# Two sparse graph layers on one core: units interleaved by an order that a list of operations makes, over both layers

## The chip, the cores and the metric

The kernel runs on one core of one Trainium2 chip. The metric is the device time of one execution in microseconds, the median of several runs. The profile is one execution on the same kind of chip.

## The reference

There are 2708 nodes with 128 features and a 0/1 adjacency matrix. Its entry (i, j) is drawn with a probability that falls as 1/sqrt((1+i)(1+j)), so the first rows and columns hold most of some 11000 edges. The matrix is dense in memory, 29 MB of float32.

```python
# layer 0: attention over the edges, 4 heads of 32
q, k, v = x @ Wq + bq, x @ Wk + bk, x @ Wv + bv          # by heads
alpha = softmax over the edges of a row of (q . k) / sqrt(32)   # 0 where a row has no edge
out = alpha @ v                                           # by heads, laid out (c, h)
x_r = x @ Ws + bs
beta = sigmoid(concat(out, x_r, out - x_r) @ Wb)
x = layernorm(x + beta * x_r + (1 - beta) * out)
# layer 1: messages over the edges
s, d = x @ msg_w[:, :128].T, x @ msg_w[:, 128:].T
aggregated[i] = sum over edges (i, j) of gelu(s[i] + d[j] + msg_b) * adj[i, j]
h = gelu(concat(x, aggregated) @ upd_w.T + upd_b) + x
x = layernorm(x + layernorm(h) * ln_w + ln_b)
```

## The kernel before

The kernel has a sparse path, `sparse_layers`, and a dense path that runs only if a flag says that some list was too short (more edges in a row or segment than there are slots). The sparse path finds the edges of the adjacency matrix and works edge by edge.

Rows are taken in 22 blocks of R = 126. `plan` cuts the columns of a block into segments in which a row is expected to have few edges, and makes units: block 0 gives three units (a part of the columns each), every other block one, 24 in all. A unit has a number of slots per row (64 in block 0, then 24 or 16) and a number of chunks of 128 edges, 110 in all.

- Start: x is loaded (on the ACT queue), transposed into `xT` by blocks, and multiplied by `wtab`. The result is the table `kv_t` in DRAM, one row of 264 numbers per node: key, and for each head 32 values, a one (for the sum of the weights) and the value's share in the gate.
- `load(b)`: the block's 126 rows of the adjacency matrix come into one of three buffers `abuf` on the SP queue. The buffer's two last partitions hold the column numbers in two parts.
- `keys(b)`: ACT reads the whole buffer as 16-bit numbers to add them up (L654, for the flag). PE multiplies it by `lkey` in pieces of 512 columns (L663), so that each entry is the column number plus 2^20 where there is an edge. The DVE takes the eight largest of each segment (`max`, L667).
- `place(u)`: the candidates of a row are cleaned and sorted by rounds of `max` and `match_replace` (L690, L692). A product with `before` (L696) gives the number of edges in the rows above, so each row owns an interval of edge positions. Two DVE passes (L707, L708) write a 0/1 matrix `t32` whose column e is one where the row owns edge e; ACT casts it to bf16 into `T16` (L710) for later. A product with it (L714) brings each edge its row's query, slots and first position; the DVE picks the slot (L717 to L724) and the index `idx` is there. POOL gathers the rows of `kv_t`, one gather for 128 edges (L728). PE transposes the bf16 matrix (L738), and ACT copies it twice (L741, L742), as `s32` and into `S`.
- `attend(b)`: product of query and key on the DVE (L753), sum by head (L754), exp on ACT (L757), weighted values on the DVE (L759), and a product with `s32` adds them up by row (L765).
- `finish(gi)`: for a group of up to three blocks, division by the sums, gate, residual and layernorm, with a reciprocal square root by shifts and three Newton steps on the DVE (L846 to L852). Then transposes (L816), a product with two weights (L823), a copy to `dv` (L826) that is stored to the table `d_t` in DRAM on the SP queue (L828), and `sv` (L827).
- `message(b)`, layer 1: POOL gathers rows of `d_t` (L906). ACT casts `T16` and `S` back to f32 (L911, L913). A product brings each edge its row's `sv` (L916), the DVE adds (L919), ACT does the gelu (L920), and a product with `s32` adds up by row (L922).
- `update(b, at)`: for each block on its own, two products (L952, L953), gelu, two layernorms with the same Newton steps for one column each (L932 to L939, normalised on the DVE, L947), and a store (L963).

The calls stand in a loop over the blocks (`keys(b)`, then `attend(b - 1)`), then a loop of `update(b, message(b))`. The framework decides the order of the instructions on each engine from that program; each engine then runs its own list in order and waits on semaphores. POOL's queue holds the gathers, SP's the adjacency blocks and the stores of `d_t` and the output, ACT's the stores of `kv_t`.

Of the kernel before, what the change touches and what calls it, by code (L numbers as in the profile page):

```python
# [9 lines left out]
F32 = mybir.dt.float32  # L10
# [5 lines left out]
P = 128  # L16
BANK = 512
# [393 lines left out]

# [6 lines left out]
HV = 34  # L418
RSQRT = float(0x5F3759DF)


def plan(N):

    w = [(1.0 + i) ** -0.5 for i in range(N)]
    total = sum(w)
    units = []
    for b in range(-(-N // R)):
        lam = 4.0 * w[b * R] * N / total  # L430
        edges = 4.0 * N / total * sum(w[b * R : (b + 1) * R])
        n = 3 if b == 0 else 1
        most = min(0.26, 1.4 / lam)
        segments, at, acc = [], 0, 0.0
        for j in range(N):
            acc += w[j] / total
            edge = (j + 1) % KT == 0 or j + 1 == N
            if edge or (acc >= 0.97 * most and j + 1 - at >= CAP and KT - (j + 1) % KT >= CAP and N - j > 64):
                segments.append((at, j + 1, acc))
                at, acc = j + 1, 0.0  # L440
        group, weight = [], 0.0
        for i, (s0, s1, share) in enumerate(segments):
            group.append((s0, s1))
            weight += share
            if i + 1 == len(segments) or (weight >= 0.97 / n and len(units) < n - 1 and b == 0):
                lu, eu = lam * weight, edges * weight
                slots = -(-int(lu + 4.2 * math.sqrt(lu) + 2.5) // 8) * 8
                chunks = int(math.ceil((eu + 3.5 * math.sqrt(eu)) / P))
                units.append((b, group, slots, chunks))
                group, weight = [], 0.0  # L450
    return units
# [3 lines left out]
def sparse_layers(ctx, tc, flag, x, adj, wq, bq, wk, bk, wv, bv, ws, bs, wb, msg_w, msg_b, upd_w,  # L455
                  upd_b, ln_w, ln_b, out):

    nc = tc.nc
    N, D = x.shape
    C = D // HEADS
    NB = (N + R - 1) // R
    scale = 1.0 / math.sqrt(C)
    rows_of = [min(R, N - b * R) for b in range(NB)]
    full = N // R
    units = plan(N)  # L480
    NU = len(units)
    NCH = sum(u[3] for u in units)
    chunk0 = [sum(u[3] for u in units[:i]) for i in range(NU)]
    most_chunks = max(u[3] for u in units)
    most_slots = max(u[2] for u in units)
    TW = D + HEADS * HV
    U16, U32, I32 = mybir.dt.uint16, mybir.dt.uint32, mybir.dt.int32

    def bcast(v, n):
        return v.rearrange("(o d) -> o d", o=1).to_broadcast([P, n])  # L490

    const = ctx.enter_context(tc.tile_pool(name="fconst", bufs=1))
    dram = ctx.enter_context(tc.tile_pool(name="fdram", bufs=1, space=bass.MemoryType.DRAM))
# [3 lines left out]
    xs = const.tile([P, NB, D], F32, name="xs")  # L497
    nc.scalar.dma_start(xs[:R, :full, :], x[: full * R, :].rearrange("(t p) d -> p t d", p=R))
    nc.scalar.dma_start(xs[: N - full * R, full, :], x[full * R :, :])
    wkv = const.tile([P, 2, D], F32, name="wkv")  # L500
    wqs = const.tile([P, 2 * D + 1], F32, name="wqs")
    bkv = const.tile([P, 2, D], F32, name="bkv")
    bqs = const.tile([P, 2 * D + 1], F32, name="bqs")
    nc.scalar.dma_start(wkv[:, 0, :], wk)
    nc.scalar.dma_start(wkv[:, 1, :], wv)
    nc.gpsimd.dma_start(bkv[:, 0, :], bcast(bk, D))
    nc.gpsimd.dma_start(bkv[:, 1, :], bcast(bv, D))
    wb3 = const.tile([P, 3, D], F32, name="wb3")
    nc.gpsimd.dma_start(wb3.rearrange("p a d -> p (a d)"), bcast(wb.rearrange("k o -> (k o)"), 3 * D))
    nc.scalar.dma_start(wqs[:, :D], wq)  # L510
    nc.scalar.dma_start(wqs[:, D : 2 * D], ws)
    nc.gpsimd.dma_start(bqs[:, :D], bcast(bq, D))
    nc.gpsimd.dma_start(bqs[:, D : 2 * D], bcast(bs, D))

    ident = const.tile([P, P], F32, name="fident")
    make_identity(nc, ident)
    ident16 = const.tile([P, P], BF16, name="ident16")
    nc.vector.tensor_copy(ident16, ident)

    lkey = const.tile([P, P], BF16, name="lkey")  # L520
    nc.vector.tensor_scalar(lkey, ident, BIG, None, op0=ALU.mult)

    NADJ = 3
    abuf = [const.tile([P, N], F32, name=f"abuf{i}") for i in range(NADJ)]
    pidx = const.tile([P, 1], F32, name="pidx")
    iota = const.tile([P, most_chunks * P], F32, name="iota")
    dcol = const.tile([P, most_chunks], F32, name="dcol")
    before = const.tile([P, P], BF16, name="before")
    with tc.tile_pool(name="ftmp", bufs=1) as tmp:
        cnum = tmp.tile([1, 2, N], F32, name="cnum")  # L530
        cint = tmp.tile([1, N], I32, name="cint")
        nc.gpsimd.iota(cint, [[1, N]], base=1, channel_multiplier=0)
        nc.vector.tensor_copy(cnum[:, 0, :], cint)
        nc.vector.tensor_single_scalar(cint, cint, 63, op=ALU.bitwise_and)
        nc.vector.tensor_copy(cnum[:, 1, :], cint)
        nc.vector.tensor_sub(cnum[:, 0, :], cnum[:, 0, :], cnum[:, 1, :])
        ones_row = tmp.tile([1, P], BF16, name="ones_row")
        nc.vector.memset(ones_row, 1.0)

        nc.sync.dma_start(lkey[R : R + 1, :], ones_row)  # L540
        nc.sync.dma_start(lkey[R + 1 : R + 2, :], ones_row)
        for a in abuf:
            nc.sync.dma_start(a[R : R + 1, :], cnum[:, 0, :])
            nc.sync.dma_start(a[R + 1 : R + 2, :], cnum[:, 1, :])
        ii = tmp.tile([P, most_chunks * P], I32, name="ii")
        nc.gpsimd.iota(ii, [[1, most_chunks * P]], base=0, channel_multiplier=0)
        nc.vector.tensor_copy(iota, ii)
        di = tmp.tile([P, most_chunks], I32, name="di")
        nc.gpsimd.iota(di, [[P, most_chunks]], base=0, channel_multiplier=1)
        nc.vector.tensor_copy(dcol, di)  # L550
        nc.vector.tensor_copy(pidx, dcol[:, 0:1])

        nc.vector.tensor_scalar(before, iota[:, :P], pidx, None, op0=ALU.is_gt)

    def load(b):
        rows = rows_of[b]
        nc.sync.dma_start(abuf[b % NADJ][:rows], adj[b * R : b * R + rows, :])

    for b in range(NADJ - 1):
        load(b)  # L560

    w_l1 = const.tile([P, 4, D], F32, name="fw_l1")
    nc.gpsimd.dma_start(w_l1[:, 0:2, :], msg_w.rearrange("o (h k) -> o h k", h=2))
    nc.gpsimd.dma_start(w_l1[:, 2:4, :], upd_w.rearrange("o (h k) -> o h k", h=2))
    vecs = const.tile([P, 4, D], F32, name="vecs")
    for i, v in enumerate((msg_b, upd_b, ln_w, ln_b)):
        nc.gpsimd.dma_start(vecs[:, i, :], bcast(v, D))


    xT = const.tile([P, N], F32, name="fxT")  # L570
    bits = const.tile([P, NB], F32, name="bits")
    count = const.tile([P, NU], F32, name="count")
    ends = const.tile([P, NU], F32, name="ends")
    caps = const.tile([P, 2, NU], F32, name="caps")
    for t in (bits, count, ends):
        nc.vector.memset(t, 0.0)
    for u in range(NU):
        nc.vector.memset(caps[:, 0, u : u + 1], float(units[u][2]))
        nc.vector.memset(caps[:, 1, u : u + 1], float(units[u][3] * P))
    idx = const.tile([P, NCH], U32, name="idx")  # L580
    score = const.tile([P, NCH, HEADS], F32, name="score")
    T16 = const.tile([P, NCH * P], BF16, name="T16")
    S = const.tile([P, NCH, R], BF16, name="S")
    sv = const.tile([P, NB, D], F32, name="sv")
    wT = const.tile([P, 4, D], F32, name="fwT")

    wtab = const.tile([P, TW], F32, name="wtab")
    btab = const.tile([P, TW], F32, name="btab")  # L590
    wg = const.tile([P, 2, D], F32, name="wg")
    nc.vector.tensor_add(wg[:, 0, :], wb3[:, 0, :], wb3[:, 2, :])
    nc.vector.tensor_sub(wg[:, 1, :], wb3[:, 1, :], wb3[:, 2, :])
    wA = wg[:, 0, :].rearrange("p (c h) -> p h c", h=HEADS)
    with tc.tile_pool(name="ftmp2", bufs=2) as tmp:
        for src, dst, one in ((wkv, wtab, 0.0), (bkv, btab, 1.0)):
            nc.vector.tensor_copy(dst[:, :D], src[:, 0, :])
            v = src[:, 1, :].rearrange("p (h c) -> p h c", h=HEADS)
            t = dst[:, D:].rearrange("p (h c) -> p h c", c=HV)
            nc.vector.tensor_copy(t[:, :, :C], v)  # L600
            nc.vector.memset(t[:, :, C : C + 1], one)
            pr = tmp.tile([P, HEADS, C], F32, name="pr")
# [407 lines left out]
```

## Time and profile before

| what | value |
|---|---|
| time, median of 3 runs | 802.68 us (801.0 to 806.31) |
| span of the profiled execution, first to last instruction | 778.9 us |
| that execution's own time | the page gives the span alone |
| from the start to the first gather of layer 0 | 88.2 us |
| from there to the first gather of layer 1 | 460.4 us |
| from there to the end | 230.3 us |
| mean granted TensorE clock | 0.616 |

The span runs from the first to the last instruction on the core; the time holds the launch too. Busy time of an engine is the time in which at least one of its instructions ran. "PEld" is the loading of weights into TensorE, which overlaps the products. The granted clock is the share of full speed that TensorE was given. In the list of waits, "POOL g L728 <- DVE rq L690: 99.4, 2, 74.0" reads: the instruction of line 728 on POOL, which writes g, waited 99.4 us in all, 2 times, at the longest 74.0, for the instruction of line 690 on the DVE.

### The profile page before, as it was taken

How to read it: one execution, taken by the hardware profiler on the slowest of the kernel's cores; microseconds unless marked ns; L12 is line 12 of the kernel's file. 1: busy time of each engine (PE TensorE's matmuls, PEld its weight loads, DVE VectorE, ACT ScalarE, POOL GpSimd, SP SyncE). 2: the span in 40 equal slices, each digit the busy share in tenths (PEclk: the TensorE clock that was granted, in tenths of full speed). 3: DMA queues.
4: the chain of work that ended last, by engine and by line, in shares of the span. 5: the costliest groups of instructions: out<-in, count | busy, mean ns of one | idle time of the engine just before them, and what ended most of it. 6: DMA issues, size and time to landing. Idle time of an engine off the chain costs nothing. (4 is left out here: it accounts for less than half of the span.)

```text
span 778.9 us, 6687 instructions
## 1 busy us (share of the span) xinstructions
PE 375.0 (48%) x1416; PEld 266.9 (34%) x1416; DVE 458.3 (59%) x2345; ACT 259.0 (33%) x479; POOL 220.3 (28%) x240
## 2 busy tenths in 40 slices
PE   0367467454546444454454254443456665543310
PEld 0233356233434232233232132332456654433210
DVE  1596787665656555665665545647114543667895
ACT  0293534344424523524523241122243433211000
POOL 5000234332052032032022013030677777340000
PEclk9975556565555565555555556555586776755555
DMA  8346112453143243234234102020122223111000
GB/s 237 112 146 202 54 49 64 137 165 107 29 139 112 75 125 99 77 94 135 78 93 126 34 17 56 11 49 19 42 55 50 61 56 59 34 37 23 14 15 12
DMA packets 24700, 60.29 MB, mean 77 GB/s; under 512 B 5050, under 2 KB 16396, under 8 KB 21940
## 3 DMA queue, kind: packets, MB, share of 16 engines
q0 software_dynamic: 9216, 23.08, 12.9%
q1 hardware_dynamic: 9128, 32.18, 12.9%
q10 hardware_dynamic: 6304, 4.51, 2.0%
q14 instruction: 39, 0.32, 0.1%
q8 instruction: 13, 0.21, 0.1%
HBM read 54.04 MB, written 5.63 MB: 77 GB/s over the span
## 5 line engine op out<-in xcount | busy, mean ns | idle before, releaser
L728 POOL DMA_INDIRECT g<-kv_t,idx x110 | 106.2, 966 | 405.4 <-DVE rq L690 99.4
L906 POOL DMA_INDIRECT gd<-d_t,idx x110 | 103.9, 944 | 80.2 <-issue 31.6
L654 ACT ACTIVATE junk<-abuf 126x5416 uint8<-126x5416 uint16 (+1 forms) x22 | 103.7, 4713 | 51.6 <-DMA abuf<-in_adj_dram 32.0
L663 PE MATMUL pk<-abuf,lkey 128*128 128x512 bf16 x132 | 64.1, 516 | 64.2 <-DVE cand L667 54.3
L765 PE MATMUL pr<-val,s 128*126 128x136 f32 (+1 forms) x220 | 59.7, 436 | 69.0 <-DVE val L759 51.2
L667 DVE MAX8 cand<-pk 128x8 f32<-128x512 f32 (+23 forms) x223 | 87.8, 429 | 0.1
L714 PE MATMUL pq<-rq,t 126*128 126x145 f32 (+3 forms) x220 | 67.8, 467 | 35.1 <-DVE t L708 27.7
L765 PEld LDWEIGHTS pr<-val,s 128*126 128x126 f32 (+1 forms) x220 | 49.6, 309 | 98.8 <-DVE val L759 82.3
L753 DVE TENSOR_TENSOR qe<-qe,g 128x384 f32<-128x384 f32 (+2 forms) x48 | 22.0, 462 | 85.5 <-DMA g<-kv_t,idx 85.4
L919 DVE TENSOR_TENSOR gd<-gd,pz 128x512 f32<-128x512 f32 (+3 forms) x34 | 19.9, 585 | 88.5 <-DMA gd<-d_t,idx 82.6
L916 PE MATMUL pz<-sv,t32b 126*128 126x128 f32 (+1 forms) x220 | 48.4, 375 | 46.9 <-DVE gd L919 30.9
L714 PEld LDWEIGHTS pq<-rq,t 126*128 126x128 f32 (+1 forms) x220 | 53.5, 311 | 45.8 <-DVE t L708 22.3
L916 PEld LDWEIGHTS pz<-sv,t32b 126*128 126x128 f32 (+1 forms) x220 | 41.4, 273 | 53.1 <-DVE gd L919 27.1
L922 PE MATMUL pa<-s32b,gd 128*128 128x126 f32 (+1 forms) x220 | 45.0, 367 | 12.2 <-ACT gd L920 9.7
L922 PEld LDWEIGHTS pa<-s32b,gd 128*128 128x128 f32 x220 | 40.4, 273 | 15.2 <-ACT gd L920 11.8
L663 PEld LDWEIGHTS <-lkey 128*128 128x128 bf16 x132 | 15.3, 122 | 82.9 <-issue 57.4
L920 ACT ACTIVATE gd<-gd 128x512 f32<-128x512 f32 (+3 forms) x34 | 18.6, 548 | 68.8 <-DVE gd L919 65.1
L757 ACT ACTIVATE e<-score 128x12 f32<-128x12 f32 (+2 forms) x48 | 10.0, 220 | 93.5 <-DVE score L754 65.6
L827 DVE TENSOR_TENSOR sv<-pm,vecs 126x128 f32<-126x128 f32 (+1 forms) x22 | 6.4, 291 | 45.5 <-ACT dv L826 45.5
L952 PE MATMUL pn<-fwT,fxT 128*126 128x128 f32 (+1 forms) x44 | 14.6, 436 | 38.1 <-DVE h L955 31.6
L823 PE MATMUL pm<-fwT,fxT 128*126 128x256 f32 (+1 forms) x44 | 23.0, 682 | 20.7 <-ACT fxT L819 20.7
L710 ACT CAST T<-t 126x384 bf16<-126x384 f32 (+3 forms) x48 | 20.0, 437 | 36.2 <-DVE t L708 35.8
(162 smaller groups left out, 756.2 us busy)
## 6 DMA issues: line engine op xcount, KB each, us to landing
abuf<-in_adj_dram SPq DMA_DIRECT2D x21, 1332.8 KB
kv_t<-kv ACTq DMA_DIRECT2D x21, 129.9 KB
g<-kv_t,idx POOLq DMA_INDIRECT x110, 3.0
gd<-d_t,idx POOLq DMA_INDIRECT x110, 2.6
xs<-in_x_dram ACTq DMA_DIRECT2D x1, 1323.0 KB
d_t<-dv SPq DMA_DIRECT2D x21, 63.0 KB
out_dram<-h SPq DMA_DIRECT2D x21, 63.0 KB
abuf<-in_adj_dram SPq DMA_DIRECT2D x1, 655.8 KB
```

The costliest lines, as they stand in the source:

```text
L654: nc.scalar.activation(junk[:rows], a.bitcast(U16)[:rows], AF.Copy, accum_out=bits[:rows, b : b + 1])
L663: nc.tensor.matmul(p[:, :n], lkey, low[:, 2 * c0 + 1 : 2 * (c0 + n) : 2], start=True, stop=True)
L667: nc.vector.max(cand[u][:, i * CAP : (i + 1) * CAP], p[:, s0 - c0 : s1 - c0])
L710: nc.scalar.copy(T16[:rows, (ch + c0) * P : (ch + c0 + m) * P], t32[:rows, : m * P])
L714: nc.tensor.matmul(pq[:, (c - c0) * W : (c - c0 + 1) * W], t32[:rows, (c - c0) * P : (c - c0 + 1) * P], rq[:rows, :W], start=True, stop=True)
L728: nc.gpsimd.indirect_dma_start(out=g[:, c, :], out_offset=None, in_=kv_t[:, :], in_offset=bass.IndirectOffsetOnAxis(ap=idx[:, ch + c0 + c ...
L753: nc.vector.tensor_tensor(qe[:, :m, :], qe[:, :m, :], g[:, :m, :D], ALU.mult)
L765: nc.tensor.matmul(pr[:rows], s32[:, c, :rows], val[:, c, :], start=ch + c == parts[0][0], stop=ch + c == last)
L823: nc.tensor.matmul(pt[:r, : 2 * D], xT[:, b * R : b * R + r], wT[:, 0:2, :].rearrange("p a d -> p (a d)"), start=True, stop=True)
L906: nc.gpsimd.indirect_dma_start(out=g[:, c, :], out_offset=None, in_=d_t[:, :], in_offset=bass.IndirectOffsetOnAxis(ap=idx[:, ch + c : ch + ...
L916: nc.tensor.matmul(pz[:, c * D : (c + 1) * D], t32[:rows, c * P : (c + 1) * P], sv[:rows, b, :], start=True, stop=True)
L922: nc.tensor.matmul(pa[:, :rows], g[:, c, :], s32[:, c, :rows], start=ch + c == mine[0][0], stop=ch + c == last)
```

## The change

`plan` and `sparse_layers` are written anew; the dense path and the switch stay.

- Order. Every operation is first put on a list by `add(engine, ns, function, r=..., w=...)`, with an estimated duration and the names that it reads and writes. `Order.emit` then walks through time: on each engine it takes, of the operations that can start soonest (within 30 ns), the one with the longest chain of estimated work behind it, with 100 ns for each step from one engine to another, and calls the functions in order of the planned starts. The framework keeps that order (`manual_schedule`). The list covers both layers, with fixed buffers and the eight PSUM banks by name; one of them, "MI", is lent to one short step after another.
- Sign steps. Instead of a 0/1 matrix by two DVE passes, `E` is Sign(position + 1/2 - first position of the row), one ACT activation per unit, in f32, with -1 left of the row's first edge and +1 right of it. Everything that is spread over edges by a product with `E` is first turned into differences of neighbouring rows: the slots by a product with `dif`, the queries by `dx` (differences of `xT`'s columns) and half weights, with the bias from a bf16 product of three parts. The row matrix `S32` comes from a product of `E` with `difs` and stays in f32 for both layers; `E` is made again in layer 1. The bf16 copies `T16` and `S`, their transposes and casts are gone.
- Virtual rows. Block 0 has 109 rows. Its 15 heaviest are split by columns into 8 virtual rows each, the next 31 into 4, the next 63 into 2: three units of up to 126 virtual rows, with 32, 24 and 24 slots, and 22 segments in place of 73. The split is a sum of T products over columns t, t + T, ... with shifted copies of `lkey`.
- Groups. Chunks (109) are worked on four at a time across units in `spread`, `attend` and `message`; the selection takes up to 9 chunks at once. Blocks are finished and updated in 9 groups. The table of layer 0 has 260 columns, stored by 7 DMAs; `d_t` and the output are stored by 9 DMAs each. x is loaded first on the SP queue.
- Smaller. In layer 0 the reciprocal square root is exp(-ln/2) on ACT with one Newton step; normalising is done on ACT; the sum of gate and residual and the differences of the new `xT` are done on POOL; in layer 1 the products with `sv`'s weights are made by unit in `skip`.

The core of the diff:

```diff
+HEAVY = ((0, 15, 8), (15, 46, 4), (46, 109, 2))
...
+class Order:
+    HAND = 100.0
...
+                t, p = min(((t, p) for t, p in seen if t <= soon + 30.0), key=lambda s: (-s[1].height, s[1].i))
...
+        for p in sorted(ops, key=lambda p: (p.start, p.i)):
+            p.fn()
...
-                nc.vector.tensor_scalar(after[:rows, : m * P], here, rq[:rows, D + K : D + K + 1], None, op0=ALU.is_ge)
-                nc.vector.scalar_tensor_tensor(t32[:rows, : m * P], here, ends[:rows, u : u + 1],
-                                               after[:rows, : m * P], op0=ALU.is_lt, op1=ALU.mult)
-                nc.scalar.copy(T16[:rows, (ch + c0) * P : (ch + c0 + m) * P], t32[:rows, : m * P])
...
-                    nc.tensor.transpose(pt[:, c * P : c * P + rows], T16[:rows, o : o + P], ident16[:rows, :rows])
...
+        def stepsign(u):
...
+                add("ACT", ac(m * P), lambda c=c, s=s, m=m: A.activation(
+                    E[:, s : s + m, :].rearrange("p c e -> p (c e)"), half[:, c * P : (c + m) * P], AF.Sign,
+                    bias=dsl[:, u.i, 0:1]), r=["half", ("dsl", u.i)], w=[("E", (s + k) % RING) for k in range(m)])
...
+            add("PE", 300, lambda: T_.matmul(mi.ap[:, 2 : 2 + K], dif, rs[:, :K], start=True, stop=True),
+                r=["dif", "dif_", rk], w=[mi])
+            add("ACT", ac(K), lambda: A.copy(dsl[:, i, : K + 2], mi.ap[:, : K + 2]), r=[mi, "dsl"], w=[("dsl", i)])
+            stepsign(u)
...
+                    add("PE", pe(K + 1) + 100, lambda u=u, o=o, c=c: T_.matmul(
+                        view[:, o, :], E[:, (u.c0 + c) % RING, :], dsl[:, u.i, 1 : K + 2], start=True, stop=True),
...
+        def spread(q):
...
+                add("PE", pe(128), lambda j=j, u=u: T_.matmul(
+                    bank[kq][:, j * D : (j + 1) * D], E[:, (c0 + j) % RING, :], dq[u.i % NQ], start=True, stop=True),
...
+                add("PE", pe(R), lambda j=j, sel=sel: T_.matmul(
+                    bank["SS"][:, j * R : (j + 1) * R], E[:, (c0 + j) % RING, :], sel, start=True, stop=True),
...
+            add("ACT", ac(m * R), lambda: A.copy(S32[:, c0 * R : (c0 + m) * R], bank["SS"][:, : m * R]),
...
+            add("POOL", po(n * 128), lambda: G.tensor_tensor(gx[:r, :n, :], gx[:r, :n, :], xs[:r, b0 : b0 + n, :], ALU.add),
...
-        for b in range(NB):
-            if b + NADJ - 1 < NB:
-                load(b + NADJ - 1)
-            keys(b)
-            if b:
-                attend(b - 1)
-        attend(NB - 1)
...
+        for j, bt in enumerate(batches):
+            for u in bt:
...
+                scan(u)
+                place(u)
+            select(j)
+            upto = bt[-1].c0 + bt[-1].nch
+            while 4 * done_q + 4 <= upto or (upto == NCH and 4 * done_q < NCH):
+                spread(done_q)
+                attend(done_q)
+                done_q += 1
...
-    for b in range(NB):
-        update(b, message(b))
...
+        for q in range(-(-NCH // 4)):
+            message(q)
...
+        add.emit({"MI": [bank["MI"]]})
```

## The prediction

> **What bounds the kernel now.** I read the page's head first, then the busy time by stage, then the waits, then single stretches of the timeline. No engine is full:
>
> ```profile
> span 778.9 us, 6687 instructions
> PE 375.0 (48%) x1416; PEld 266.9 (34%) x1416; DVE 458.3 (59%) x2345; ACT 259.0 (33%) x479; POOL 220.3 (28%) x240
> ```
>
> Busy time is the union. The durations of the 2345 DVE instructions add up to 600.3 us, so each overlaps its neighbour by 142.0 / 2345 = 0.061 us; below I take that off every DVE instruction that I count. The median of the runs is 802.68 us, 23.8 us above this execution's span; the page gives no other time for that execution, so I sum against the span and add 23.8.
>
> I cut the span at the first gather of layer 0 (88.2 us) and of layer 1 (548.6 us):
>
> ```profile
> 0.00:88.20 88.20, 39.61 (x109) 21.31 (x109) 49.03 (x258) 36.39 (x30) 10.25 (x20) 0.81 0.52 156
> 88.20:548.60 460.40, 229.73 (x796) 153.24 (x797) 280.10 (x1262) 167.37 (x333) 106.26 (x111) 0.57 0.28 82
> 548.60:778.90 230.30, 105.64 (x514) 92.40 (x513) 129.16 (x826) 55.28 (x119) 103.83 (x110) 0.63 0.18 38
> ```
>
> Columns: window, its length, busy PE, PEld, DVE, ACT, POOL, granted clock, DMA share, GB/s. In layer 0 the DVE is busy 280.1 / 460.4 = 61% and nothing else is busier. The waits say why:
>
> ```profile
> POOL g L728 <- DVE rq L690: 99.4, 2, 74.0
> DVE qe L753 <- DMA g<-kv_t,idx: 85.4, 33, 7.4
> DVE gd L919 <- DMA gd<-d_t,idx: 82.6, 28, 9.1
> DVE sv L827 <- ACT dv L826: 45.5, 22, 14.2
> DVE kk L717 <- PE pq L714: 24.4, 30, 2.7
> ```
>
> The gathers wait for the DVE, which makes the indices, and the DVE waits for the gathers: 85 us in layer 0, although POOL has work for only 106 of 460 us. It is a matter of order. The order is better where many units are at hand, in the densest 60 us of layer 0, with the DVE at 48.75 / 60 = 81%:
>
> ```profile
> 80.00:100.00 20.00, 9.29 (x33) 6.81 (x31) 16.89 (x85) 9.59 (x22) 5.76 (x6) 0.50 0.17 45
> 100.00:120.00 20.00, 13.96 (x53) 11.81 (x54) 16.54 (x78) 7.34 (x28) 7.60 (x8) 0.62 0.23 54
> 120.00:140.00 20.00, 13.35 (x59) 10.30 (x60) 15.32 (x67) 8.28 (x26) 11.87 (x13) 0.73 0.33 81
> ```
>
> Layer 1 has two parts: gathers one after another (a start every 1.25 us, first two lines below), then a tail of updates on the DVE alone:
>
> ```profile
> 571.04 0.94 POOL L906 DMA_INDIRECT gd<-d_t,idx  x1 [0.30 <-issue]
> 572.29 0.94 POOL L906 DMA_INDIRECT gd<-d_t,idx  x1 [0.30 <-issue]
> ...
> 573.24 1.16 PE L916 MATMUL pz<-sv,t32b 126*128 126x128 f32 x8 [2.33 <-DVE gd L919]
> ...
> 636.26 1.91 PE L922 MATMUL pa<-s32b,gd 128*128 128x126 f32 x8
> ...
> 688.27 0.79 PE L952 MATMUL pn<-fwT,fxT 128*126 128x128 f32 x2 [2.31 <-DVE h L955]
> ```
>
> ```profile
> 680.00:778.90 98.90, 28.05 (x106) 22.51 (x104) 75.52 (x531) 8.63 (x23) 11.33 (x12) 0.52 0.09 20
> ```
>
> An f32 product leaves two PE records, so the PE lines price one: 1.16 / 4 = 0.29 us in a row at clock 1.00, 1.91 / 4 = 0.48 at 0.50, 0.79 alone.
>
> **The change: the start.** Before, 88.2 us pass until the first gather: x is queued on ACT while SP has adjacency blocks in flight (its first transpose starts at 23.9), and the 22 rows of the key/value table wait for buffers and for the keys' 73 narrow maxima of block 0. After, x goes first on SP, the adjacency blocks wait for small row transfers, the table rows have room of their own, and its 22 stores on the ACT queue become 7. The DVE has 90 instructions ahead of and including the first index, 32.1 us by the rows (22 table additions at 0.425 are 9.4 of it; a 1x2708 cast of 1.55 becomes 4x677), less 90 x 0.061: 27 us. PE has beside it 22 transposes (5.1 us by L632), 22 table products (20.4 by L641) and the first scans: 32 us. PE cannot begin before x is there. x is 1.39 MB; the first 20 us of before moved 238 GB/s, so 6 us and about 4 until transposed. So the first index is at 10 + 32 + 3 (select) = 45, the first gather at 47. Bounds: 38 (DVE and PE overlap wholly) to 60 (table rows wait as before).
>
> **Layer 0.** Removed: the two interval passes per group of chunks (L707, L708, 17 and 24 us), the cast to T16 (20), the bf16 transposes (L738, 110 products) and their two copies (20 each). Added: one Sign activation per unit for E. No row is a Sign; as an ACT pass of 128x512 it costs 0.61 to 0.63 (L911, L920), so 109 chunks of 128 columns are some 17 us per layer; the ends are 10 and 25. The slots, the queries and the selection then go through difference matrices, which costs PE: 109 products for S, 24 + 24 for slots and queries. The scan is unchanged in width: three virtual units of 2708 columns on PE in place of one, 174 maxima in place of 223, but mostly of the same long segments, so 88 us on the DVE again. Groups of four chunks make 28 rounds of products, scores and values (3 x 0.69 us) in place of 48 smaller ones.
> DVE from the first index to the last val: 652 instructions, 233 us of durations (scan 88, placing 32, selection 20, attention 57, block ends 28, the rest setup), less 40: 193 us, where before has 280.
> PE: 572 f32 products, where before has 286. 439 are 126 to 136 wide, at 0.29 to 0.48: 127 to 211 us. 133 have 16 to 33 columns; no row is so narrow, so half of those prices to all of the upper one: 19 to 64, I take 32 at the half clock. Scans, 127 pieces of 512 columns at 0.28 to 0.53 (L663: 1.06 for two at half clock): 36 to 67. 94 small bf16 products at 0.15 to 0.2: 14 to 19. Sum 196 us at the full clock, 329 at half.
> ACT: 22 reads of the adjacency at 4.9 (L654) are 108, plus Sign 17, copies of S 17 and smaller things: 172. Here is the new wait: the copy of a unit's slots, its Sign and the exp stand in ACT's queue with these reads, and one behind a read holds the PSUM bank MI and PE's next products up to 4.9 us. Uncovered that is 22 x 4.9 = 108 us; other units' maxima and products cover it, as ACT's and DVE's work on other units covers most of the 65.6 us that exp (L757) waits now. POOL: 109 gathers x 1.25 = 136, plus 18 additions and differences that were DVE work. No row is such an addition; between 0.28 (the 128x128 select of the identity) and 1.08 us (the 128x1152 iota, L546) each: 5 to 19, I take 14.
> So the four engines need 193, 196 to 329, 172 and 150 us, and PE's clock decides. Now the clock:
>
> ```profile
> 584.00:588.00 4.00, 2.59 (x12) 0.50 0.33 55
> 588.00:592.00 4.00, 4.00 (x21) 0.50 0.21 52
> 592.00:596.00 4.00, 3.03 (x21) 0.85 0.25 46
> ```
>
> Four full microseconds of PE and the clock rises. With twice the products PE is full more often. I put two thirds of the work at the full clock: about 240 us, and 265 for the stretch (PE 91%, DVE 73%, between its 61% and 81%). Ends: 193 / 0.81 = 238, and PE at half clock, 329 / 0.93 = 354. In the new order of the DVE's instructions 10 to 50 us of its own work lie between an index and the first use of its gather, more than the waits of 7.4 at most, so the 85 us go to nearly nothing; the 45 us for dv go because nobody on the DVE waits for that copy any more.
> The Trainium skill ("TensorE: Matmul & The Clock Gate", section on the HAM clock gate) has a half clock until a window of about 3.4 us is busy, and again after an idle one. The three rows agree. By that rule alone a fuller PE would stay at the full clock, which is the second rival below.
> The last val to the first gather of layer 1 took 17.1 us (531.5 to 548.6); the chain of block end, transpose, product, store is as long: 17. The stores are 9, not 22, on the SP queue behind the last adjacency load.
> The Trainium skill ("SBUF — State Buffer", section on who interferes with whom) says that a DVE instruction with two SBUF inputs and a POOL instruction that reads SBUF shut each other out. The gathers show no such thing (966 ns in layer 0, 944 in layer 1), but POOL's additions are new; by the rule up to 14 us would be added.
>
> **Layer 1.** 109 gathers x 1.25 = 136 us. The casts of T16 and S (18 us each on ACT) go, Sign (17) and 24 rows through PE and ACT come. DVE: 432 instructions, 97.5 - 26 = 71 us, since 22 updates become 9 and the normalising goes to ACT. PE 286 products at 0.29 to 0.48 and small ones: 90 to 150. Both lie under the gathers, unless PE stays at half clock: then 150 is more than 136. The tail is the last two groups: landing 2.3, addition, gelu, six products, two normalisations of about 3, store 2.5: 18. Sum with 3 us of start: 157; ends 148 and 190.
>
> **Sum:** 47 + 265 + 17 + 157 = 486, and 23.8: 510 us.
>
> **Rivals.**
> PE is the bound and its clock stays where layer 0 has it, 0.57. Then 329 - 0.14 x 133 = 310 us of PE, 93% full: 333, layer 1 at 165: 47 + 333 + 17 + 165 + 24 = 586. For it: idle gaps of 2 to 3 us between products everywhere. Against: those gaps are waits for the DVE, which has less to do. PE stays at the full clock: 196 us of work, so the DVE at 81% sets layer 0: 47 + 238 + 17 + 157 + 24 = 483, and 465 with the low ends of the start and of layer 1. For it: 0.85 and 1.00 after the full stretch above. Against: the clock was back at 0.51 by 600 us, after a stretch with PE at 39%.
> Slower than before: products cannot be lined up, since each follows a copy by ACT or a DVE step and one PSUM bank (MI) is lent to one step at a time. A product alone takes 0.79 (L952) and about 0.2 to hand over: 572 x 1.0 + 86 = 658, total 47 + 658 + 17 + 165 + 24 = 911. It decides from 0.83 us per product on, where layer 0 reaches 558. Against: spread, S and attention go by fours, and bursts of eight records are everywhere.
> The change does not do what it says: the flag is raised and the dense layers run too. Their 2708 gelus over 2708 columns alone, at 630 ns for 512, are over 8000 us. Against: the counting is only re-encoded.
>
> **How the numbers follow.** My sum 0.62, PE at a low clock 0.20, PE at the full clock 0.12, products alone 0.04, the flag 0.01, no gain for a cause that I have not seen 0.01. The range 455 to 625 leaves out the last three, the worse part of the second and the DVE above 81%. 1% is about what can be told from no change: faster 0.94, same 0.01, slower 0.05.
>
> **What would show it.** First gather near 47; DVE busy near 291 us over the span in some 1180 instructions; PE busy above before's in layer 0 with a clock above 0.57; the DVE's wait for g under 20 us; gathers of layer 1 every 1.25 us for 136 us and 20 us after the last. If the span of layer 0 is over 330 and PE's clock is low, the second case holds; if PE and DVE both stand idle there, the order is bad and my sum is wrong.

## The result and the profile after

The changed kernel takes 647.12 us (642.82 to 649.3, 4 runs), the kernel before beside it 803.4 (801.0 to 806.31): a ratio of 0.8061, 95% interval 0.8019 to 0.8103. It is faster, as forecast, but the time lies above the range of 455 to 625. Ratios here are taken over fast runs alone (those within 1.5% of the fastest of their kernel), so they can differ a little from the quotient of two medians.

The page of the changed kernel, its head and the busy time of DVE in 40 slices of 16.2 us:

```profile
span 647.4 us, 6658 instructions
PE 388.4 (60%) x2013; PEld 319.1 (49%) x2013; DVE 335.5 (52%) x1229; ACT 252.7 (39%) x425; POOL 235.3 (36%) x307
...
DVE  7500075477758858876405876621105032665665
```

DVE has half of its instructions left and 335.5 us in place of 458.3. But its row has two holes ahead of layer 1, in slices 3 to 5 and in slice 21 (two more zeros, 30 and 32, lie in layer 1). The stretches, cut at the first gather of each layer, and the holes (columns as before: window, length, busy PE, PEld, DVE, ACT, POOL, clock, DMA share, GB/s):

```profile
0.00:99.00 99.00, 30.16 (x113) 17.62 (x113) 36.09 (x117) 7.46 (x14) 9.38 (x64) 0.69 0.31 93
99.00:436.30 337.30, 242.31 (x1338) 202.89 (x1338) 214.26 (x722) 185.91 (x284) 122.75 (x135) 0.76 0.42 123
436.30:647.40 211.10, 115.96 (x562) 98.55 (x562) 85.19 (x391) 59.37 (x128) 103.21 (x109) 0.64 0.19 42
...
60.00:80.00 20.00, 2.66 (x5) 0.64 (x6) 0.00 (x0) 0.00 (x0) 0.00 (x0) 0.50 0.06 27
320.00:340.00 20.00, 0.65 (x1) 0.14 (x1) 0.00 (x0) 0.71 (x1) 0.00 (x0) 0.51 0.06 25
```

In both holes every engine stands nearly still, and the DMA share is 0.06, one engine of sixteen, at 25 to 27 GB/s. The waits, lines left out, name the transfer:

```profile
POOL gk L994 <- DVE cand L921: 95.6, 2, 88.9
PE pKA L917 <- DMA abuf<-in_adj_dram: 77.8, 2, 54.3
DVE cand L921 <- PE pKA L917: 64.4, 11, 56.4
DVE h L1238 <- ACT h L1236: 53.3, 6, 23.1
...
ACT E L961 <- remote: 20.9, 3, 16.7
```

PE waits twice for a load of the adjacency, 54.3 us for block 0 and 23.6 for the last block; DVE waits for PE, and POOL's first gather for DVE. The two blocks have 109 and 79 rows, the 20 others 126. DVE's 85 us of waiting for layer 0's gathers is gone from the list, as forecast. Two other lines are new: DVE at an update's sum for ACT (L1238), and waits "remote", which are let go by an event that no record explains (a record is the entry of one instruction in the trace).

### The profile page after: what moved, and what is told of

Same layout as the page of the kernel before. It is cut to its first block, busy times and chain, and to the rows that moved or that the text cites. A ratio compares the mean times of both kernels' runs of the same rounds, so it can differ in the third digit from the quotient of the medians.

```text
span 647.4 us, 6658 instructions
## 1 busy us (share of the span) xinstructions
PE 388.4 (60%) x2013; PEld 319.1 (49%) x2013; DVE 335.5 (52%) x1229; ACT 252.7 (39%) x425; POOL 235.3 (36%) x307
## 3 DMA queue, kind: packets, MB, share of 16 engines
q0 software_dynamic: 8880, 22.06, 14.4%
## 5 line engine op out<-in xcount | busy, mean ns | idle before, releaser
L994 POOL DMA_INDIRECT gk<-kv_t,idx x109 | 107.1, 983 | 220.1 <-DVE cand L921 95.6
L1186 POOL DMA_INDIRECT gk<-d_t,idx x109 | 103.2, 947 | 71.1 <-issue 32.4
L901 ACT ACTIVATE junk<-abuf 126x5416 uint8<-126x5416 uint16 (+2 forms) x22 | 103.8, 4719 | 50.7 <-DMA abuf<-in_adj_dram 39.2
L921 DVE MAX8 cand<-pKA 126x8 f32<-126x512 f32 (+14 forms) x100 | 48.4, 500 | 77.4 <-PE pKA L917 64.4
L961 ACT ACTIVATE E<-half,dsl 128x512 f32<-128x512 f32 (+6 forms) x54 | 39.0, 723 | 39.8 <-remote 20.9
L917 PE MATMUL pKA<-abuf,lkey 128*126 128x512 bf16 (+1 forms) x63 | 29.6, 470 | 41.1 <-DMA abuf<-in_adj_dram 23.6
L1010 PE MATMUL pSS<-difs,E 128*128 128x126 f32 x218 | 47.3, 336 | 9.3 <-ACT S L1013 8.2
L1041 PE MATMUL pAG<-val,S 128*126 128x136 f32 (+2 forms) x218 | 46.4, 331 | 5.4 <-ACT fsums L1090 4.2
L1041 PEld LDWEIGHTS pAG<-val,S 128*126 128x126 f32 (+2 forms) x218 | 38.9, 226 | 18.6 <-issue 6.9
L1010 PEld LDWEIGHTS pSS<-difs,E 128*128 128x128 f32 x218 | 39.2, 235 | 17.6 <-ACT S L1013 9.7
L1004 PE MATMUL pQ<-dq,E 128*128 128x128 f32 x218 | 45.0, 335 | 3.3 <-ACT dq L954 3.3
L1238 DVE TENSOR_TENSOR h<-h,xs 126x384 f32<-126x384 f32 (+3 forms) x9 | 4.3, 483 | 71.4 <-ACT h L1236 53.3
L917 PE MATMUL pKA<-abuf,base 128*128 128x339 bf16 (+3 forms) x14 | 7.6, 671 | 54.3 <-DMA abuf<-in_adj_dram 54.3
L917 PEld LDWEIGHTS <-lkey 128*126 128x126 bf16 (+1 forms) x126 | 20.2, 164 | 29.9 <-DMA abuf<-in_adj_dram 23.8
```

The source lines that it names most:

```text
L901: add("ACT", 4900, lambda: A.activation(junk[:r], abuf[i].bitcast(U16)[:r], AF.Copy, accum_out=bits[:r, b : b + 1]), r=[("a", i), "bits"], ...
L917: add("PE", pe(cols, False), lambda o=o, lhs=lhs, rhs=rhs, t=t, T=T: T_.matmul(o, lhs, rhs, start=t == 0, stop=t == T - 1), r=[("a", i), " ...
L921: add("DVE", 150 + 1.04 * (s1 - s0), lambda cd=cd, j=j, k=k, s0=s0, s1=s1, c0=c0, n=n: V.max(cd[:n, j * CAP : (j + 1) * CAP], bank[k][:n, ...
L961: add("ACT", ac(m * P), lambda c=c, s=s, m=m: A.activation(E[:, s : s + m, :].rearrange("p c e -> p (c e)"), half[:, c * P : (c + m) * P], ...
L994: add("POOL", 1250, lambda c=c, gt=gt: G.indirect_dma_start(out=gt[:, c % 4, :], out_offset=None, in_=kv_t[:, :], in_offset=bass.IndirectO ...
L1004: add("PE", pe(128), lambda j=j, u=u: T_.matmul(bank[kq][:, j * D : (j + 1) * D], E[:, (c0 + j) % RING, :], dq[u.i % NQ], start=True, stop ...
```

## The experiments

Each kernel ran beside the kernel before on one chip. The batches ran on different chips, and the kernel before takes 796 us on three of them and 774 on one, so kernels of different batches are compared by their ratio to it. Line numbers of the kernels below lie up to five above the changed kernel's.

### The two loads

```diff
-add("LD", 4500, lambda: nc.sync.dma_start(abuf[i][:r], adj[a0[b] : a0[b] + r, :]),
+cuts = {109: (0, 96, 109), 79: (0, 64, 79)}.get(r, (0, r))
+add("LD", 4500, lambda: [nc.sync.dma_start(abuf[i][p:q], adj[a0[b] + p : a0[b] + q, :])
+                         for p, q in zip(cuts, cuts[1:])],
```

> The changed kernel, with two of its 22 loads of the adjacency each sent as two transfers: block 0's 109 rows as 96 and 13, the last block's 79 rows as 64 and 15. Nothing else is changed, and the order of all instructions stays. Theory (a transfer is shared out over as many DMA engines as divide its row count, so 109 and 79 rows, both prime, go through one engine of sixteen): the two waits of PE for a load, 54.3 and 23.6 us, go; the load of block 0 lands some 5 us after its issue instead of 51; span about 570, first gather at 47 to 55 us. Rival (the load is late because other transfers stand before it on SP's queue or in the memory): both waits stay, span 640 to 650. The Trainium skill, DMA: Bandwidth & Descriptors, How many engines (k), states the theory's rule, the largest number up to 16 that divides the slowest dimension; by it 96, 13, 64 and 15 rows go over 16, 13, 16 and 15 engines.

For `two_engines` the cuts are (0, 106, 109) and (0, 74, 79). For `more_rows` there are none, and block 0 reads `abuf[i][:126]`.

> The changed kernel, with block 0's load reading 126 rows of the adjacency in place of 109, in one transfer (the 17 extra rows have zero weights in the products, so they change nothing); the last block's load stays as it was. Theory (row count decides the number of engines: 126 has the divisor 14, 109 none): 16% more bytes land some 45 us earlier, PE's wait of 54.3 us goes and the one of 23.6 stays, span about 600. Rival (bytes or a queue decide): block 0 lands no earlier, or 16% later, span 645 to 655.

> The changed kernel, with the 109 rows sent as 106 and 3 and the 79 rows as 74 and 5. 106 is 2 x 53 and 74 is 2 x 37, so by the theory these pieces go over two engines: block 0 takes half of its 51 us, about 26, PE's two waits shrink from 54.3 to about 28 and from 23.6 to about 6, and the span is about 605. If splitting a load helps for another reason (two requests in flight, a shorter transfer), it lands as early as in the kernel with 96 and 13 rows, span about 570. If a queue decides, nothing moves: 640 to 650.

The other way round, in the kernel before:

```diff
-nc.sync.dma_start(abuf[b % NADJ][:rows], adj[b * R : b * R + rows, :])
+cuts = (0, 109, R) if b == 0 else (0, rows)
+for p, q in zip(cuts, cuts[1:]):
+    nc.sync.dma_start(abuf[b % NADJ][p:q], adj[b * R + p : b * R + q, :])
```

> The kernel before, with its block 0's load of 126 rows sent as 109 and 17. Theory (a prime row count goes through one engine): the 109 rows take about 50 us instead of a few, the scan of block 0 starts at 50 to 60 us instead of about 40, and the span grows from about 779 to 790 to 815. Rival (a queue decides): two requests in place of one change nothing, 775 to 785.

Measured: with both loads split 577.12 us (ratio 0.718, 0.7119 to 0.7241); one run each with more rows, 604.12, over two engines, 605.72, and of the kernel before with 109 rows, 841.75, beside 795.8 unchanged. The first product on block 0, in the timeline of the changed kernel, then of the one with 126 rows, then over two engines (start, duration, and in brackets the wait ahead of it):

```profile
77.34 5.02 PE L917 MATMUL pKA<-abuf,base 128*128 128x339 bf16 x8 [54.28 <-DMA abuf<-in_adj_dram]
```

```profile
37.15 5.03 PE L918 MATMUL pKA<-abuf,base 128*128 128x339 bf16 x8 [13.28 <-DMA abuf<-in_adj_dram]
```

```profile
56.37 5.03 PE L919 MATMUL pKA<-abuf,base 128*128 128x339 bf16 x8 [32.33 <-DMA abuf<-in_adj_dram]
```

All are issued at 25.9 to 26.0 us. 109 rows take 51.4 us until they are used, 126 rows in one transfer 11.2, though they are 16% more bytes; 106 and 3 rows take 30.4, and 96 and 13 take 10.2 (first product at 36.2). The last block's wait is 23.6, 24.1 (not touched there), 7.7 and none. The row count decides, not the bytes or a queue, and the dose fits: with 106 and 3 rows the load takes 0.6 of the time, and from 45 to 56 us, all engines idle, the DMA share is 0.13 at 53 GB/s, twice the figures of the holes. The Trainium skill ("DMA: Bandwidth & Descriptors", section "Why a DMA increments its semaphore by 16 and not by 1") states it: a transfer goes over the largest number of engines up to 16 that divides its slowest dimension. The traces agree; 109 and 79 are prime.

In the kernel before the same cut costs 46 us, more than I expected, and by another way. Its timeline of busy time and its waits:

```profile
40.00:60.00 20.00, 0.00 (x0) 0.00 (x0) 0.00 (x0) 0.00 (x0) 0.00 (x0) 1.00 0.06 26
```

```profile
PE pm L634 <- DMA xs<-in_x_dram: 65.2, 1, 65.2
```

There it is x that lands at 65 us instead of 24, a transfer on another queue. Until then one engine of sixteen is busy, so what is missing of x must stand on the engine that the 109 rows fill (inferred from the share; the trace does not name the engine). In the changed kernel x stands ahead of the block on SP.

### Layer 1: buffers, order, prices, gathers

With split loads layer 1 still takes 211.8 us (first gather at 366.5, span 578.3), where I had 157. Four kernels, each with split loads:

```diff
 # ring8
-gt, gi = gk[q % NG], q % NG
+gt, gi = gk1[q % len(gk1)], q % len(gk1)      # gk1: gk and four views of abuf
 # late_updates: the same three steps of update()
-..., r=[ka], w=[ak])
+..., r=[ka], w=[ak], late=2500)
 # plan_costs
-HAND = 100.0; pe: 60.0 + 1.9 * n; ve: 150.0 + 0.85 * n; ac: 190.0 + 0.62 * n
+HAND = 400.0; pe: 60.0 + 2.8 * n; ve: 90.0 + 1.05 * n;  ac: 165.0 + 0.87 * n
 # plain_loads
-add("POOL", 1250, ... G.indirect_dma_start(out=gt[:, j, :D], ..., in_=d_t[:, :], ...
+add("SP", 1250, ... nc.sync.dma_start(gt[:, j, :D], d_t[1 + c * 20 : 1 + c * 20 + P, :]), ...
```

> The kernel with both loads split (span 578.3), and in layer 1 eight buffers for groups of gathers in place of four: the four new ones lie in the adjacency's buffers, which are free by then. Theory (buffers: layer 1's gathers, which take 168 us for 109 x 1.25 = 136 us of work, stand still because a buffer comes free only when the products over the group four before it are done): the gathers take 136 to 145 us, and the end moves up by most of that, span 550 to 560. Rival (the engines behind the gathers set the pace: DVE's additions queue behind an update's sum that waits for ACT, 58.9 us in six waits, and products complete late): the gathers run ahead, the additions come as late as before, span 570 to 580.

> The kernel with both loads split, and in the planner's costs 2.5 us more between the steps of a layer-1 update that go from ACT to PE, PE to ACT and ACT to DVE; no instruction is added or taken away, but DVE's sum of an update is put behind one or two more additions of gathered rows. Theory (head-of-line: DVE stands at that sum for 58.9 us in six waits while gathered rows are there to be added): these waits fall under 20 us, the gathers take 145 to 155 us instead of 168, span 555 to 568. Rival (products complete late, whatever stands in DVE's queue): the waits move to the additions, span 572 to 582.

> The kernel with both loads split, and the planner's prices changed to what the trace shows: a wide f32 product 0.42 us at 128 columns (it had 0.30), DVE 0.63 at 512 (0.585), ACT 0.61 at 512 (0.51), a handover between engines 0.4 us (0.1). Theory (the order is planned with prices that are too low for PE, so its queues stand in the wrong order in both layers): layer 0 from the first gather to layer 1's first takes 285 to 300 us instead of 308, layer 1's gathers 150 to 160, span 540 to 565. Rival (the order is about as good as it can be, the waits come from products that complete late and from the depth of the chains): 570 to 585.

> The kernel with both loads split, and in layer 1 the 109 gathers by index replaced by 109 plain loads of 128 neighbouring rows on SP's queue (so layer 1 works on other rows than it should; shapes, sizes and all other instructions stay). In layer 1 of the kernel with split loads, ACT, DVE and POOL wait some 55 us for products whose records had ended up to 13 us before. Theory A (the index gathers hold the products' completion up): without them these waits, marked as remote, go in layer 1, and its 168 us shrink to 110 to 130, set by PE. Theory B (PE itself, by its clock or its code): they stay at 30 to 55 us with no gather running.

Measured: eight buffers 598.51 us (0.7495, 0.7424 to 0.7566), so slower, which neither theory had; late updates 575.82 (0.7204, 0.7137 to 0.7272) and new prices 579.76 (0.7221, 0.7147 to 0.7295), no change; plain loads 522.09, their 109 loads in 105 us.

The theory of the head of line falls: with late updates DVE's wait at the sum went from 58.9 to 20.6 us, but the gathers took 166.0 us as against 168.2, and ACT's remote wait ahead of L1178 rose from 18.2 to 41.0. That the order is planned with wrong prices falls too, as far as the new prices go. The kernel with eight buffers shows what the remote waits are. Its timeline, ACT, PE and POOL, lines left out:

```profile
386.62 1.09 PE L1199 MATMUL pKB<-dq,E 128*128 128x128 f32 x4
387.51 1.06 PE L1199 MATMUL pQ<-dq,E 128*128 128x128 f32 x4
...
416.60 0.95 POOL L1191 DMA_INDIRECT gk<-d_t,idx  x1 [0.30 <-issue]
417.85 0.94 POOL L1191 DMA_INDIRECT gk<-d_t,idx  x1 [0.30 <-issue]
...
421.05 0.93 ACT L963 ACTIVATE E<-half,dsl 128x768 f32<-128x768 f32 x1 [36.31 <-remote]
```

In the program this Sign waits for one thing, the pKB product of the first line, which reads the chunk of E that Sign overwrites. Its records end at 387.7; Sign starts at 421.05, 33 us later, 2.3 us after POOL's last gather of an unbroken row (369.0 to 418.8, every 1.25 us). In these 33 us PE is busy for 0.9 us and DVE for 1.4. The same pair in the changed kernel is 454.2 and 467.93. So what waits for a product can be let go long after the product's record, while index gathers follow each other; I call such products late. With eight buffers the row of gathers and the longest wait are longer (36.3 us against 14.7 with four), but the remote waits of layer 1 add up to about the same (56.6 and 52.7 us). So that the longer row costs the time of the eight buffers is only argued; the order of all instructions is planned anew in each of these kernels, which is a rival. The Trainium skill ("Perfetto Trace Analysis", section on the Tensor Engine instruction) says that a record of TensorE begins when data is fetched and that its end is computed, not seen. The trace fits this: the record ended at 387.7 us, and what waited for it began at 421.05. With plain loads layer 1 has no remote wait at all.

### Fewer buffers, and another chip

```diff
 # ring3, ring2
-gt, gi = gk[q % NG], q % NG
+gt, gi = gk[q % 3], q % 3       # ring2: 2
 # paced
+add("POOL", 1250, ... (G.memset(abuf[c % 2][:, :1000], 0.0), G.memset(gt[:, j, :D], 0.0)), ...
+add("SP", 100, ... nc.sync.dma_start(gt[:, j, :D], d_t[1 + c * 20 : 1 + c * 20 + P, :]), ...
 # newton2
-for _ in range(1 if logs else 3):
+for _ in range(1 if logs else 2):
```

> The kernel with both loads split, with three buffers for groups of gathers in layer 1 in place of four. New theory, from eight buffers being 4% slower and plain loads having no such waits: while index gathers follow each other without a pause, products of PE complete late (with eight buffers, ACT stood 36.3 us for a product whose record had long ended, and was let go 2.2 us after POOL's last gather); fewer buffers mean earlier pauses. By it three buffers are no slower and may be faster, median 560 to 577, with the waits marked as remote in layer 1 under 20 us instead of some 40. Rival (buffers are what layer 1 lacks): slower, 582 to 600.

> The kernel with both loads split, with two buffers for groups of gathers in layer 1. A group of four gathers takes 5 us, and from its last gather until its buffer is free again pass about 2 us of transfer, 0.7 of addition, 0.6 of gelu and 2 of products. By the new theory the remote waits in layer 1 go (under 10 us), and layer 1's gathers are set by the buffers: 28 groups at (5 + 5.5) / 2 or more, 150 to 175 us, median 565 to 590. Rival (buffers are what layer 1 lacks): 28 groups at 7 to 8 us, 195 to 225, median 605 to 635.

> The kernel with both loads split; in layer 1 POOL fills memory for about 1.2 us per chunk in place of each gather by index, and then SP loads 128 neighbouring rows, so the rows come at about the pace of the gathers but without one (layer 1 works on other rows than it should). It parts the two things that the plain loads took away, the pace and the gathers. If the gathers hold the products' completion up: no remote waits in layer 1, its loads take 136 to 145 us at the pace of POOL, span 540 to 555. If it was the pace alone that plain loads changed: remote waits of 30 to 55 us stay, loads 160 to 170 us, span 570 to 585.

> The kernel with both loads split, with two steps in place of three of the reciprocal square root on DVE in the layer-1 updates: 18 chains of 15 small instructions lose three each, at 0.196 us from start to start. Theory (the 44 us after the last gather are DVE's chains for the last updates, one after the other: some seven of them stand there): 7 x 3 x 0.196 = 4 us off the tail, at most 10.6 in all; median 567 to 575. Rival (the tail is set by ACT, PE and the store of the rows): no change, 575 to 580.

Measured: 537.3 us (0.692, 0.6859 to 0.6981), 540.8 (no interval), 536.17 and 527.84 (0.6802, 0.6744 to 0.6861). But the kernel before took 773.56 here, and no kernel of this batch has a single remote wait, in either layer, not even newton2, which keeps four buffers and all gathers. Its gathers of layer 1:

```profile
L1188 POOL DMA_INDIRECT gk<-d_t,idx x109: 940/945/1299, 354.6 to 490.7; - x109
```

136.1 us for 109, where the changed kernel has 436.3 to 601.9, 165.6. So this batch could not answer its questions; it raised another: is it the chip or the edit?

### The unchanged kernels beside the combined ones

`best` has split loads and two root steps, and its adjacency loads no longer stand behind the row transfers:

```diff
-r=["cnum0", "cnum1"], w=[("ci", i, h), ("a", i)], late=2500)
+r=["cnum0", "cnum1", "am0"], w=[("ci", i, h)], late=2500)   # and scan() reads ("ci", i, h)
```

> The changed kernel, unchanged, beside the kernel with split loads on one chip. If late products belong to the chip: where none are seen, its layer-1 gathers take 136 to 142 us in place of 166, and the median is 600 to 615; where they are seen, 640 to 650. In both cases some 70 us more than with split loads.

> The kernel with both loads split, as it ran before at 577. If late products belong to the chip and this one has none: no waits marked as remote, layer-1 gathers 136 to 142 us, median 530 to 540. If they belong to the kernel (and three buffers, or two root steps, took them away): waits of some 40 us in layer 1 again, gathers 165 us, and about 4% slower than the kernel with two root steps was against the kernel before, a ratio of 0.71 to 0.72.

> Both loads split, two root steps in place of three, and at the start the loads of the adjacency no longer queued on SP behind the six small row transfers, which take SP from 14 to 26 us (the transfers of the small rows wait for DVE; the first products wait for both now). Expected: first gather at 47 to 52 us instead of 57, two root steps 4 to 10 us, median 10 to 18 us under the kernel with split loads beside it. If the table of keys and values, not the adjacency, sets the first gather, the start stays at 55 to 58 and only the 4 to 10 us are left.

> The same with three buffers for groups of gathers in layer 1. Where products complete late: 10 to 40 us faster than with four, since POOL pauses earlier. Where none do: within 1% of four buffers, at most some us slower.

Measured, beside 796.66 for the kernel before: the changed kernel 640.86 (0.8062, 0.7975 to 0.8149), split loads 573.91 (0.721, 0.7109 to 0.731), best 575.64 (0.7234, 0.7116 to 0.7352), with three buffers 568.62 (0.7152, 0.7057 to 0.7247). All four have remote waits in layer 1: 49 us in the changed kernel, 59 with split loads, 41 in best, 47 in best with three buffers. Three buffers or two root steps had none on the other chip, so whether there are such waits depends on the chip. That three buffers make them shorter is not borne out (47 against 41), and the 7 us that three buffers gain, where I expected 10 to 40, lie within the intervals. The split is worth 67 us here. Two root steps and earlier loads show no gain, within some 10 us either way: best's first gather is at 58.1 as against 59.3, so the adjacency no longer sets it, and its tail is 44.0 as against 45.5. So most of the gain that newton2 seemed to have was the chip's.

### The last two

> The kernel with both loads split, where layer 1 has for each gather a fill of about 1.2 us on POOL and then a plain load of 128 neighbouring rows (other rows than layer 1 should have). On a chip where the kernel before takes about 796: if the gathers hold the products up, no waits marked as remote in layer 1, loads in 136 to 145 us, span 530 to 545; if the pace does, remote waits of 30 to 55 us, loads in 160 to 170 us, span 565 to 580. On a chip where it takes about 774, nothing new.

> Both loads split, two root steps, early loads, and two buffers for groups of gathers in layer 1 instead of four. On a chip where the kernel before takes about 796: if pauses of POOL let late products through, faster again than three buffers' 569, 550 to 567, a ratio of 0.69 to 0.71; if two buffers cost more in waiting than they give, 570 to 590. On a chip where it takes about 774: 525 to 540.

This chip has the kernel before at 795.64 and remote waits in layer 0 of both kernels (28 us in the paced one). In layer 1 the kernel with two buffers, which keeps its gathers, has 28 us of them, among them the line below; the paced kernel has none, and takes 557.44 us.

```profile
ACT dq L1178 <- remote: 18.9, 4, 8.5
```

So it is the index gathers, or what goes with them on POOL's queue, and not the pace. (The paced loads took 158 us, not the 136 to 145 expected; POOL stood 32 us for buffers.) Pauses of POOL do not do away with the waits: with two buffers 28 us are left. Two buffers give 566.51 us, 0.7122 (0.7085 to 0.7159): faster than the kernel before and, by 0.7122 to 0.8062, than the changed one; against split loads with four buffers (0.721) and best with three (0.7152) the intervals overlap. Why gathers hold products up on three chips and not on the fourth is open; no kernel tried an explanation.

## Why the prediction was wrong

The stretches as the prediction cut them, in us, for the changed kernel, for split loads on a chip with late products, and for newton2 (split loads and two root steps) on the chip without. The columns add up to the time of the execution:

| part | predicted | after | split_both | newton2 |
|---|---|---|---|---|
| start to the first gather | 47 | 99.0 | 58.4 | 57.2 |
| layer 0 to its last val | 265 | 312.5 | 283.7 | 272.9 |
| last val to layer 1's first gather | 17 | 24.8 | 24.4 | 24.5 |
| layer 1, first to last gather | 136 | 165.6 | 168.2 | 136.1 |
| from there to the end of the span | 21 | 45.5 | 43.6 | 38.3 |
| outside the span | 24 | 1.9 | 2.0 | 2.0 |
| sum | 510 | 649.3 | 580.3 | 531.0 |

**The step that failed is the start**, and with it the last block in layer 0. I counted x by its bytes, and PE's and DVE's work, with bounds of 38 to 60; block 0's load had no term, and its row count was not looked at, though the change makes that block 109 rows and the last one 79. The runs put 41 us on the first and 24 to 29 on the second, 67 to 70 together by the split. The page of before had a trace of it, in a line that I passed over:

```profile
ACT junk L654 <- DMA abuf<-in_adj_dram: 32.0, 8, 14.4
```

14.4 us is its last block, 62 rows in place of 126, half the bytes and the longest wait for a load; during it (434 to 449 us) the DMA share is 0.12, two engines of sixteen. Without the waits for these two loads the time is 577, inside the range, but that owes something to luck, as the next term shows.

**The term outside the span**, 23.8 us, was mis-sized. I took the distance between one execution's span and the median of others. In all runs that give both, the kernel before has 1.8 to 2.4 us there. The profiled execution of before had therefore taken about 781 (an estimate, 778.9 and 2); 774 on one chip against 796 on three is a difference of that kind. The trace of before has no remote wait, like the kernels on the chip with 774. The kernel before with 109 rows, on a chip with 796, has 103 us of them, all in layer 1:

```profile
ACT s32b L915 <- remote: 45.8, 8, 9.3
```

From its first gather of layer 1 (586.8 us) to its end it takes 252.6 us, where the page of before has 230.3. So late products meet the kernel before too, and the 22 us most likely are theirs. The term hid 22 us of other misses.

**Layer 1's gathers** came out at 136.1 us against 136 where products complete in time, and 22 to 32 us longer with four buffers elsewhere. The new term is shown to depend on the chip and on the index gathers. **The tail** is 38 to 45 us, not 21: I counted the last two groups, and DVE still has chains of earlier updates to do then, 27 of the 44 us with split loads. That DVE's chains set it is only argued, and fewer root steps did not shorten it visibly.

**Layer 0 itself** came out near its sum. With split loads, from the first gather to the last val (284 us), DVE is busy 206 us (I had 193), ACT 176 (172), PE 226 at a mean clock of 0.77. I had 240 for PE with two thirds of the work at the full clock; that is 131 us at 1.00 and 110 at 0.50, a mean of 0.77 as well. The stretch is 284 and 273 us against 265, and DVE's wait for the gathers is gone. That PE sets it is not shown: PE is busy 80% of it, where I had 91%. The gathers take 983 and 947 ns each in the changed kernel, against 966 and 944 before, so of the rule that the prediction cites, that DVE and POOL shut each other out, they show at most 2 us over 109; POOL's nine additions (L1119) take 7.7 us in all, and DVE waits 3.9 us for them. **The start without the load** is 58, not 47: by 60 us DVE has had 118 instructions, not 90, and 37 us, not 27. The chain between the layers is 24, not 17. Over the span DVE is busy 335.5 us in 1229 instructions, not 291 in 1180: with split loads 36 us in the start, 206 to the last val, 8 in the chain and 85 in layer 1, where I had 27, 193, nothing and 71.

My test for a bad order, "if PE and DVE both stand idle there, the order is bad", pointed the wrong way: they stood idle for one DMA engine. And the rival at 586 for a low clock, 0.57 in layer 0, would have looked right at 577, where layer 0 has 0.77, and so for a wrong reason.

## What to carry to other kernels

When a change alters how rows are cut into blocks, write down the row count of each transfer and its divisors up to 16; a large prime number of rows sends a megabyte through one engine, which shows in a profile as stretches with all engines idle and a DMA share of 0.06. Split such a load in two, or load a few rows more. Do not add the distance of a span to another run's time to a sum: take both from one execution, or leave it out.

## What the runs showed of the hardware

- A load of 109 rows (1153 KB) fills one DMA engine for some 45 us, an estimate at the 26 GB/s of the trace, and a transfer on another queue can be held up with it: x at 65 us instead of 24 in the kernel before.
- On three of the four chips of the experiments, what waits for a product was let go up to 33 us after the product's record while index gathers followed each other; plain loads in place of the gathers removed this from layer 1. Eight buffers for the gathers were slower than four (0.7495, 0.718). On the fourth, nothing of the kind, and the kernels are 3% (before) and 4 to 8% (with split loads) quicker.
